# Relative scores of two chunks from one PSUM bank in an attention and expert kernel

## The chip, the cores and the metric

The kernel runs on one core of a Trainium2 chip. The metric is device time in microseconds, the median of several executions. The core has a matmul engine (PE, with its weight loads shown apart as PEld), a vector engine (DVE), an activation engine (ACT), GpSimd (POOL), and a sync engine (SP) which here only issues DMAs. PE writes its results to PSUM, which has eight banks of 128 partitions x 512 fp32 values; DVE and ACT read them out ("drain" them) to SBUF.

## The reference, cut to what matters

The input is x of 2 x 2048 tokens by 256, in fp32. After a layer norm there are two branches, multiplied with each other and added to x. One is attention with relative positions, the other a layer of eight experts, one of which is chosen per token.

```python
q = proj(Wq, bq); k = proj(Wk, bk); v = proj(Wv, bv)     # 16 heads of 16
idx = jnp.clip(r[None, :] - r[:, None], -M, M) + M       # M = 128
content  = einsum('bhqd,bhkd->bhqk', q, k)
relative = einsum('bhqd,qkd->bhqk', q, rel_k[idx])
w = softmax((content + relative) / sqrt(hd))
s = (einsum('bhqk,bhkd->bhqd', w, v)
     + einsum('bhqk,qkd->bhqd', w, rel_v[idx])) @ Wo.T + bo
g = silu(experts(xn))
return x + s * g
```

The relative part depends on key minus query alone, and is constant where the distance is 128 or more.

## The kernel before

**Stages.** The kernel first does the layer norm, the choice of experts and the projections (to about 160 us), storing q, k and v in HBM. Then it runs the experts in blocks of 256 tokens (to about 504 us). The rest is attention. Its order is written out by hand: the pools are under `manual_schedule`, and each engine does its instructions in the order in which the code issues them.

**Chunks and units.** A chunk is 128 queries of a group of four heads; there are 128 chunks (`NCH`). Four chunks in a row are a unit, of which there are 32 (`NU`). The four heads of a group lie on the four 32-row groups of PE's array, so that a matmul with 32 rows for each of the four heads can run side by side.

**Band and far keys.** For a chunk, the keys of the chunk before, its own and the next (three blocks of 128) are the band, in which the distance can be less than 128. All other keys are far: there the relative part is one of two constants, which extra rows of q and k add inside the matmul. Far scores of a unit are cut into tiles of at most 512 query columns (`far_tiles`, 13 or 14 per unit); `far_scores` makes one, ACT takes its exponential (line 824), and `far_values` multiplies it with v into the bank `av`.

**The path of the relative scores.** For each chunk and head `rel_scores` (line 616) multiplies q with `relk_t`, a table of 512 columns whose first and last 128 repeat the end values, less a constant, so that the first 128 products are zero. The matmul takes the other 384 columns. A DVE copy (line 632) drains each bank into `qr`. When the four heads of a chunk are there, one DMA writes `qr` to HBM (`qr_d`, line 637) and a second reads it back with a row stride that is one shorter (`r`, line 641), which turns relative distance into key position. `band_scores` (line 650) multiplies q with the band's keys; DVE adds `r` to it, in place, and takes the row maximum (line 666), and line 678 makes the shift of the exponent of it.

**The path of the band's weights.** One chunk later `band_weights` takes the exponentials in `r` on ACT (line 689). POOL then issues two more DMAs which skew the weights back (`w_d`, line 702, and `wr`, line 704). `turn_band` and `turn_rel` transpose 128 x 128 blocks on PE into a bank `mp`, four to a bank, and copy them to SBUF (`wt`, `wrt`); `band_values` multiplies them with v and with `rel_v`. Of the three banks of `turn_band` ACT copies one (line 733) and DVE the others (line 735); of the two of `turn_rel` one each (lines 759 and 761); the result of `band_values` is copied by ACT (line 789). `put_shifts` puts a unit's shifts into rows of q before its far scores. `finish` divides by the sums, multiplies with Wo, and adds up over the four groups of heads.

**Steps.** The loop at the end of `_attention` writes each chunk as a number of steps. In a step each of the four heads issues one score matmul: a relative one, a band one, or else the next far tile of its queue; then come the drains, then the small work hung on that step (`at(k, ...)`), then far values up to a credit (`give_values`).

```python
even = [len(tiles) * (x + 1) // CB - len(tiles) * x // CB for x in range(CB)]
steps = 2 + (even[i] if U > 0 else 3)
rel_at, band_at = (0, 0, 1, 2), tuple(steps - 3 + x for x in (0, 1, 2, 2))
```

**Buffers.** PSUM: five banks for scores (`sps`), one for `av`, two for transposes and the rest (`mps`). SBUF: one buffer for `qr`, three for `r`, 18 for exponentials. The gate of the experts, silu of their output, is worked out by `gate` in chunks 2 to 11, on POOL and ACT, and stored in HBM; its buffers `yt` and `gt2` share a pool of two each.

Of the kernel before, what the change touches and what calls it, by code (L numbers as in the profile page):

```python
# [8 lines left out]
F32 = mybir.dt.float32  # L9
# [7 lines left out]
P = 128  # L17
# [17 lines left out]
def attn_moe_gate_kernel(  # L35
# [69 lines left out]
    wq_t = load("wq_t", [P, ND, D], wq.rearrange("(k p) m -> p k m", p=P))  # L105
    wk_t = load("wk_t", [P, ND, D], wk.rearrange("(k p) m -> p k m", p=P))
    wv_t = load("wv_t", [P, ND, D], wv.rearrange("(k p) m -> p k m", p=P))
    bq_t = load("bq_t", [P, ND], bq)
    bk_t = load("bk_t", [P, ND], bk)
    bvl = load("bvl", [P, HEADS, HD], bv.partition_broadcast(P))  # L110
    rkc = load("rkc", [P, 2], relk_cols)
    rve = load("rve", [P, 2, HD], relv_ends.partition_broadcast(P))

# [15 lines left out]
    with (  # L129
# [5 lines left out]
        tc.tile_pool(name="pps", bufs=4, space=PSUM) as pps,  # L135
    ):
        xnT = ln1.tile([P, ND, T], F32, name="xnT")
        xn = ln1.tile([P, NT, D], F32, name="xn")
# [367 lines left out]
    def _attention(own, again):  # L506
        accp = own.enter_context(tc.tile_pool(name="sacc", bufs=1))
        gop = own.enter_context(tc.tile_pool(name="gout", bufs=2))
        kvp = own.enter_context(tc.tile_pool(name="kv", bufs=2))
        qrp = own.enter_context(tc.tile_pool(name="qr", bufs=1))  # L510
        rp = own.enter_context(tc.tile_pool(name="r", bufs=3))
# [104 lines left out]
        def rel_scores(n, j):  # L616

            ch = chunk_of(n)
            if "qr" not in ch:
                ch["qr"] = qrp.tile([P, HG, 3 * P], F32, name="qr")  # L620
                ch["qrs"] = 0
            ps = sps.tile([P, TB], F32, name="sp")
            nc.tensor.matmul(  # L623
                ps[:, : 3 * P],
                lhsT=ch["un"]["q"][32 * j : 32 * j + 32, chunk(ch["i"])],
                rhs=relk_t[32 * j : 32 * j + 32, P:],
                start=True,
                stop=True,
            )

            def drain():
                nc.vector.tensor_copy(ch["qr"][:, j, :], ps[:, : 3 * P])  # L632
                ch["qrs"] += 1
                if ch["qrs"] < HG:
                    return
                d = qr_d[n % 3]
                nc.sync.dma_start(
                    out=d.rearrange("p (j r) -> p j r", r=TB)[:, :, P:], in_=ch["qr"]
                )
                ch["r"] = rp.tile([P, HG, 3 * P], F32, name="r")  # L640
                nc.sync.dma_start(
                    out=ch["r"],
                    in_=bass.AP(
                        d.tensor, d.offset + P - 1, [[HG * TB - 1, P], [TB, HG], [1, 3 * P]]
                    ),
                )

            return drain

        def band_scores(n, j):  # L650
# [67 lines left out]
        def turn_band(n, part):  # L718
# [30 lines left out]
        def turn_rel(n, pair):  # L749
# [4 lines left out]
            for jj in range(2):  # L754
                for a in range(2):
                    nc.tensor.transpose(ps[:, jj, a, :], ch["wr"][:, 2 * pair + jj, chunk(a)], ident)  # L756
            dst = ch["wrt"][:, 2 * pair : 2 * pair + 2, :, :]
            if pair == 0:
                nc.scalar.copy(dst, ps)
            else:  # L760
                nc.vector.tensor_copy(dst, ps)

        def band_values(n):
# [23 lines left out]
            for a in range(2):  # L787
                add(lambda j: rvd[:, a, :], lambda j: ch["wrt"][:, j, a, :], stop=(a == 1))
            nc.scalar.copy(un["band"][:, chunk(ch["i"])], ps)
            del chunks[n]  # L790
# [140 lines left out]
        for drain in [rel_scores(0, j) for j in range(HG)]:  # L931
            drain()

        values = []
# [9 lines left out]

        def give_values(share):
# [14 lines left out]
        while n < NCH or values or any(queues) or n <= NCH + 2 * CB + 1:  # L960
# [3 lines left out]
            if i == 0 and 0 < U <= NU:  # L964
                tiles = far_tiles(U - 1)
                for t in tiles:
                    exs = {}
                    for j in range(HG):
                        queues[j].append((U - 1, t, exs, step + 2, t is tiles[-1]))
                even = [len(tiles) * (x + 1) // CB - len(tiles) * x // CB for x in range(CB)]  # L970
# [159 lines left out]
```

## Time and profile before

| | |
|---|---|
| median of 3 runs | 2462.15 us (2458.62 to 2464.61) |
| profiled execution | 2431.08 us |
| its span, first to last instruction | 2429.4 us |
| mean granted PE clock | 0.978 |
| busy: PE, PEld | 2308.6 us, 1446.7 us |
| busy: ACT, DVE, POOL | 1403.8, 993.3, 415.4 us |
| moved by DMA | 498.66 MB, 205 GB/s |

A profile is one execution. Each group of its instructions has a line of the kernel, an engine, an operation and its tiles (out<-in); a number and a mean duration follow. Matmuls are pipelined and their ends are modelled, so "busy" of PE is not work at its peak. An fp32 matmul stands as two instructions. A wait is put down to the instruction that released it. Where the text gives a stretch of time, it is in microseconds from the start of the span.

### The profile page before, as it was taken

The numbers are of one execution on the slowest core, as the hardware profiler recorded it, in microseconds if no ns is written. First come the engines' busy times: TensorE is split into PE (matmuls) and PEld (weight loads), VectorE is DVE, ScalarE is ACT, GpSimd is POOL, SyncE is SP. The second block draws the span as 40 slices with busy tenths as digits, with TensorE's granted clock in tenths as the row PEclk, the third lists the DMA queues.
The fourth block names the chain that finished last, engine by engine and source line by source line (L and its number), as shares of the span: only waits on it lengthen the run. The fifth ranks groups of instructions, "written<-read, shape, count | busy, mean of one in ns | idle before, by whom it ended". The sixth has DMA issues, their size and how long they took to land.

```text
span 2429.4 us, 59289 instructions
## 1 busy us (share of the span) xinstructions
PE 2308.6 (95%) x24522; PEld 1446.7 (60%) x24522; DVE 993.3 (41%) x2533; ACT 1403.8 (58%) x2791; POOL 415.4 (17%) x580
## 2 busy tenths in 40 slices
PE   6989999969999999999999999999999999999996
PEld 5558888844555555556555555555555555655553
DVE  5210000024444554445545544554555445545441
ACT  2211111115666777777667776776777677766774
POOL 3500000005431111111111122211111111111121
PEclk8989999978999999999999999999999999999998
DMA  6765555548765665576656676766666566656652
GB/s 211 224 187 177 185 179 176 167 137 263 248 211 194 218 228 202 195 229 216 203 194 213 241 240 222 244 220 210 207 212 219 196 221 213 219 195 204 215 198 75
DMA packets 272295, 498.66 MB, mean 205 GB/s; under 512 B 33456, under 2 KB 219600, under 8 KB 271504
## 3 DMA queue, kind: packets, MB, share of 16 engines
q1 hardware_dynamic: 218784, 304.67, 38.9%
q0 software_dynamic: 40720, 178.05, 21.2%
q10 hardware_dynamic: 12512, 12.06, 1.4%
q8 instruction: 195, 3.19, 0.6%
q14 instruction: 84, 0.69, 0.1%
HBM read 254.33 MB, written 240.39 MB: 204 GB/s over the span
## 4 chain that ended last, share of the span: by engine, by line
PE 88%; DMA 4%; DVE 3%; issue 2%; ACT 1%; POOL 1%; SPq 0%; DVEq 0%; POOLq 0%; ACTq 0%
PE sp L814 26%; PE av L834 15%; PE mp L775 7%; PE hp L476 7%; PE mp L730 7%; PE yp L487 7%; PE mp L756 5%; PE sp L656 3%; PE mp L899 2%; PE pp L317 2%; PE sp L623 2%; DVE qr L632 1%; PE pp L345 1%; DMA qr_d<-qr 1%; DMA r<-qr_d 1%
## 5 line engine op out<-in xcount | busy, mean ns | idle before, releaser
L824 ACT ACTIVATE ex<-sp 128x512 f32<-128x512 f32 (+1 forms) x1728 | 900.6, 588 | 500.3 <-PE sp L814 461.9
L814 PE MATMUL sp<-q,kT 32*128 32x512 f32 (+7 forms) x4096 | 833.6, 557 | 1.4 <-DVE qr L632 1.4
L666 DVE CUSTOM_DVE_ANT_0 r<-sp,r 128x384 f32<-128x384 f32 (+1 forms) x512 | 266.0, 539 | 538.6 <-PE sp L814 487.4
L814 PEld LDWEIGHTS sp<-q,kT 31*128 31x128 f32 (+1 forms) x4096 | 329.2, 184 | 209.5 <-issue 144.6
L834 PE MATMUL av<-ex,v 128*17 128x256 f32 (+2 forms) x7168 | 421.4, 367 | 0.0
L632 DVE COPY qr<-sp 128x384 f32<-128x384 f32 x512 | 272.6, 554 | 311.0 <-PE sp L814 265.4
L623 PE MATMUL sp<-relk_t,q 32*128 32x384 f32 x1024 | 372.6, 548 | 13.4 <-DVE stat L666 10.5
L656 PE MATMUL sp<-kT,q 31*128 31x384 f32 (+1 forms) x1024 | 356.6, 530 | 3.4 <-DVE qr L632 3.1
L834 PEld LDWEIGHTS av<-ex,v 128*17 128x17 f32 (+1 forms) x7168 | 190.5, 97 | 215.0 <-issue 108.7
L689 ACT ACTIVATE r<-r,shift 128x384 f32<-128x384 f32 (+1 forms) x512 | 294.4, 602 | 19.2 <-DVE shift L678 19.2
L730 PEld LDWEIGHTS mp<-ident,r 128*128 128x128 f32 x1472 | 159.8, 142 | 167.0 <-issue 101.0
L730 PE MATMUL mp<-ident,r 128*128 128x128 f32 x1472 | 218.1, 284 | 16.2 <-ACT r L689 16.1
L704 POOL DMA_DIRECT2D wr<-w_d x128 | 97.5, 762 | 694.6 <-PE sp L814 138.0
L483 ACT ACTIVATE hT<-hp 128x512 f32<-128x512 f32 x92 | 54.9, 597 | 271.8 <-PE hp L476 271.7
L702 POOL DMA_DIRECT2D w_d<-r x128 | 71.1, 555 | 636.9 <-ACT r L689 629.7
L476 PE MATMUL hp<-xsT,w_t 128*128 128x256 f32 x736 | 165.9, 384 | 6.0 <-DVE xsT L470 6.0
L735 DVE COPY wt<-mp 128x512 f32<-128x512 f32 x240 | 164.0, 683 | 10.7 <-PE mp L730 7.4
L487 PE MATMUL yp<-w_t,hT 128*128 128x256 f32 x736 | 162.6, 379 | 0.0
L756 PEld LDWEIGHTS mp<-ident,wr 128*128 128x128 f32 x1024 | 111.4, 142 | 79.9 <-issue 52.3
L476 PEld LDWEIGHTS hp<-xsT,w_t 128*128 128x128 f32 x736 | 140.4, 192 | 27.9 <-DVE xsT L470 8.6
L756 PE MATMUL mp<-ident,wr 128*128 128x128 f32 x1024 | 142.5, 283 | 10.3 <-DMA wr<-w_d 8.9
L487 PEld LDWEIGHTS yp<-w_t,hT 128*128 128x128 f32 x736 | 140.0, 190 | 18.9
(162 smaller groups left out, 2005.4 us busy)
## 6 DMA issues: line engine op xcount, KB each, us to landing
qr_d<-qr SPq DMA_DIRECT2D x128, 768.0 KB
r<-qr_d SPq DMA_DIRECT2D x128, 768.0 KB
w_d<-r POOLq DMA_DIRECT2D x128, 768.0 KB, 5.3
wr<-w_d POOLq DMA_DIRECT2D x128, 512.0 KB, 4.6
w_t<-in_w_dram SPq DMA_DIRECT2D x46, 1024.0 KB
xs_d<-zrow SPq DMA_DIRECT2D x23, 256.0 KB
xs<-xs_d ACTq DMA_DIRECT2D x23, 256.0 KB
ys_d<-ys ACTq DMA_DIRECT2D x23, 256.0 KB
```

Of the source, the lines that this page charges most:

```text
L476: nc.tensor.matmul(ps[:, n, :], lhsT=w1_t[:, k, (h + n) * P : (h + n + 1) * P], rhs=xsT[:, k, :], start=(k == 0), stop=(k == ND - 1),)
L487: nc.tensor.matmul(yp[:, a, :], lhsT=hT[:, h, a * P : (a + 1) * P], rhs=w2_t[:, h, :], start=(h == 0), stop=(h == NH - 1),)
L623: nc.tensor.matmul(ps[:, : 3 * P], lhsT=ch["un"]["q"][32 * j : 32 * j + 32, chunk(ch["i"])], rhs=relk_t[32 * j : 32 * j + 32, P:], start=True,
L632: nc.vector.tensor_copy(ch["qr"][:, j, :], ps[:, : 3 * P])
L656: nc.tensor.matmul(ps[:, :bw], lhsT=ch["un"]["q"][32 * j : 32 * j + RIGHT, chunk(ch["i"])], rhs=ch["gr"]["kT"][32 * j : 32 * j + RIGHT, ch ...
L666: nc.vector.tensor_tensor_reduce(out=r, in0=ps[:, :bw], in1=r, scale=1.0, scalar=LOW, op0=ALU.add, op1=ALU.max, accum_out=stat[:, n, j, 0:1],)
L689: nc.scalar.activation(r[:, j, f0 * P : f1 * P], r[:, j, f0 * P : f1 * P], AF.Exp, bias=shifts[n % (2 * CB)][:, j, ONE : ONE + 1],)
L730: nc.tensor.transpose(ps[:, x, :], ch["r"][:, j, chunk(f0 + f)], ident)
L756: nc.tensor.transpose(ps[:, jj, a, :], ch["wr"][:, 2 * pair + jj, chunk(a)], ident)
L814: nc.tensor.matmul(ps[:, at : at + e - a], lhsT=kT[32 * j : 32 * j + rows, chunk(kc)], rhs=q[32 * j : 32 * j + rows, a:e], start=True, sto ...
L824: nc.scalar.activation(exs[j][:, :n], ps[:, :n], AF.Exp)
L834: nc.tensor.matmul(un["av"][32 * j : 32 * j + cols, a:e], lhsT=v[:, kc, j, :cols], rhs=exs[j][:, at : at + e - a], start=False, stop=False ...
```

## The change

1. `rel_scores` is done for two chunks at a time. It now multiplies each chunk's q with 256 columns of `relk_t`, P to 3P, and puts the products of the two chunks into the two halves of one bank; one DVE copy drains both. It is issued at even chunks for the two chunks after the next, at steps 4, 1, 2, 3 for the four heads.
2. A new function `to_keys` fills the last 128 columns of each head in `qr` with a repeat of the column before them, on DVE, and then issues the two DMAs. It stands at step 0 of the chunk before.
3. `qr` holds two chunks and has two buffers.
4. The number of steps is changed: 2 plus far tiles at even chunks, 1 plus far tiles at odd ones. The band's matmuls stand in the last four steps, one head each. The credits of far values and the place of `load_q` are adapted.
5. DVE does the copies of turned blocks and of `band_values` that ACT did.
6. The weights of the projections, their biases and `rkc` are loaded into the pool `ln1`, which ends with the first stage; only `rve` stays in `const`. The gate's `gt2` gets a pool of one buffer.

```diff
-    def load(name, shape, src):
-        t = const.tile(shape, F32, name=name)
+    def load(name, shape, src, pool=const):
+        t = pool.tile(shape, F32, name=name)
...
-    rve = load("rve", [P, 2, HD], relv_ends.partition_broadcast(P))
+    rve = const.tile([P, 2, HD], F32, name="rve")
...
+        wq_t = load("wq_t", [P, ND, D], wq.rearrange("(k p) m -> p k m", p=P), ln1)
...
+        nc.gpsimd.dma_start(out=rve, in_=relv_ends.partition_broadcast(P))
...
+        gpp = own.enter_context(tc.tile_pool(name="gprod", bufs=1))
-        qrp = own.enter_context(tc.tile_pool(name="qr", bufs=1))
+        qrp = own.enter_context(tc.tile_pool(name="qr", bufs=2))
...
-            gt = gop.tile([P, CB * D], F32, name="gt2")
+            gt = gpp.tile([P, CB * D], F32, name="gt2")
...
             if "qr" not in ch:
-                ch["qr"] = qrp.tile([P, HG, 3 * P], F32, name="qr")
-                ch["qrs"] = 0
+                ch["qr"] = qrp.tile([P, 2, HG, 3 * P], F32, name="qr")
+                chunk_of(n + 1)["qr"] = ch["qr"]
             ps = sps.tile([P, TB], F32, name="sp")
-            nc.tensor.matmul(
-                ps[:, : 3 * P],
-                lhsT=ch["un"]["q"][32 * j : 32 * j + 32, chunk(ch["i"])],
-                rhs=relk_t[32 * j : 32 * j + 32, P:],
...
+            for x in range(2):
+                nc.tensor.matmul(
+                    ps[:, 2 * x * P : 2 * (x + 1) * P],
+                    lhsT=ch["un"]["q"][32 * j : 32 * j + 32, chunk(ch["i"] + x)],
+                    rhs=relk_t[32 * j : 32 * j + 32, P : 3 * P],
...
             def drain():
-                nc.vector.tensor_copy(ch["qr"][:, j, :], ps[:, : 3 * P])
...
+                nc.vector.tensor_copy(
+                    ch["qr"][:, :, j, : 2 * P], ps.rearrange("p (x r) -> p x r", x=2)
                 )
+        def to_keys(n):
+            ch = chunk_of(n)
+            qr = ch["qr"][:, n % 2, :, :]
+            nc.vector.tensor_copy(
+                qr[:, :, 2 * P :], qr[:, :, 2 * P - 1 : 2 * P].to_broadcast([P, HG, P])
+            )
+            d = qr_d[n % 3]
+            nc.sync.dma_start(out=d.rearrange("p (j r) -> p j r", r=TB)[:, :, P:], in_=qr)
+            ch["r"] = rp.tile([P, HG, 3 * P], F32, name="r")
+            nc.sync.dma_start(out=ch["r"], in_=bass.AP(
...
-            if part == 1:
-                nc.scalar.copy(dst, ps)
-            else:
-                nc.vector.tensor_copy(dst, ps)
+            nc.vector.tensor_copy(dst, ps)
...
+            nc.vector.tensor_copy(ch["wrt"][:, 2 * pair : 2 * pair + 2, :, :], ps)
...
-            nc.scalar.copy(un["band"][:, chunk(ch["i"])], ps)
+            nc.vector.tensor_copy(un["band"][:, chunk(ch["i"])], ps)
...
+        to_keys(0)
...
-            credit = min(credit + share, 8 * P)
+            credit = min(credit + columns, 10 * P)
...
+                share = (3, 4, 3, len(tiles) - 10)
...
-                steps = 2 + (even[i] if U > 0 else 3)
-            rel_at, band_at = (0, 0, 1, 2), tuple(steps - 3 + x for x in (0, 1, 2, 2))
+                steps = (2 - i % 2) + (share[i] if U > 0 else 3 + i % 2)
+            rel_at = (4, 1, 2, 3) if n % 2 == 0 and n + 2 < NCH else [None] * HG
+            band_at = range(steps - HG, steps)
...
-                at(2, load_q, U + 1)
+                at(0, load_q, U + 1)
...
-                at(4, turn_rel, n - 2, 0)
-                at(4, turn_rel, n - 2, 1)
+                at(min(4, steps - 1), turn_rel, n - 2, 0)
+                at(min(4, steps - 1), turn_rel, n - 2, 1)
+            if n + 1 < NCH:
+                at(0, to_keys, n + 1)
...
-                    if n + 1 < NCH and k == rel_at[j]:
-                        filled.append((1, j, rel_scores, (n + 1, j), None))
+                    if k == rel_at[j]:
+                        filled.append((1, j, rel_scores, (n + 2, j), None))
...
-                    give_values((5 if k == 1 else 7) * P)
+                    give_values((6 if k == 1 else 8) * P)
```

More of the change, by code (lines that the diff above doesn't have):

```diff
@@ L98, in attn_moe_gate_kernel @@
         nc.vector.memset(rank[:, e : e + 1], float(E - e))
-    def load(name, shape, src):
-        t = const.tile(shape, F32, name=name)
+    def load(name, shape, src, pool=const):
+        t = pool.tile(shape, F32, name=name)
         nc.gpsimd.dma_start(out=t, in_=src)
         return t
[L105 to L111, printed above, removed]
-    rve = load("rve", [P, 2, HD], relv_ends.partition_broadcast(P))
+    rve = const.tile([P, 2, HD], F32, name="rve")
     NE = T // TE + E - 1
@@ L136, in attn_moe_gate_kernel @@
     ):
+        wq_t = load("wq_t", [P, ND, D], wq.rearrange("(k p) m -> p k m", p=P), ln1)
+        wk_t = load("wk_t", [P, ND, D], wk.rearrange("(k p) m -> p k m", p=P), ln1)
+        wv_t = load("wv_t", [P, ND, D], wv.rearrange("(k p) m -> p k m", p=P), ln1)
+        bq_t = load("bq_t", [P, ND], bq, ln1)
+        bk_t = load("bk_t", [P, ND], bk, ln1)
+        bvl = load("bvl", [P, HEADS, HD], bv.partition_broadcast(P), ln1)
+        rkc = load("rkc", [P, 2], relk_cols, ln1)
+        nc.gpsimd.dma_start(out=rve, in_=relv_ends.partition_broadcast(P))
         xnT = ln1.tile([P, ND, T], F32, name="xnT")
@@ L619, in rel_scores @@
             if "qr" not in ch:
-                ch["qr"] = qrp.tile([P, HG, 3 * P], F32, name="qr")
-                ch["qrs"] = 0
+                ch["qr"] = qrp.tile([P, 2, HG, 3 * P], F32, name="qr")
+                chunk_of(n + 1)["qr"] = ch["qr"]
             ps = sps.tile([P, TB], F32, name="sp")
-            nc.tensor.matmul(
-                ps[:, : 3 * P],
-                lhsT=ch["un"]["q"][32 * j : 32 * j + 32, chunk(ch["i"])],
-                rhs=relk_t[32 * j : 32 * j + 32, P:],
-                start=True,
-                stop=True,
-            )
@@ L631, in drain @@
-            def drain():
[L632 to L645, printed above, removed]
-                )
@@ L648, in rel_scores @@
-            return drain
+            for x in range(2):
[3 more added lines that the diff above has]
+                    rhs=relk_t[32 * j : 32 * j + 32, P : 3 * P],
+                    start=True,
+                    stop=True,
+                )
+            def drain():
+                nc.vector.tensor_copy(
+                    ch["qr"][:, :, j, : 2 * P], ps.rearrange("p (x r) -> p x r", x=2)
+                )
@@ new lines, in rel_scores @@
+            return drain
+        def to_keys(n):
[3 more added lines that the diff above has]
+                qr[:, :, 2 * P :], qr[:, :, 2 * P - 1 : 2 * P].to_broadcast([P, HG, P])
+            )
+            d = qr_d[n % 3]
+            nc.sync.dma_start(out=d.rearrange("p (j r) -> p j r", r=TB)[:, :, P:], in_=qr)
+            ch["r"] = rp.tile([P, HG, 3 * P], F32, name="r")
+            nc.sync.dma_start(
+                out=ch["r"],
+                in_=bass.AP(
+                    d.tensor, d.offset + P - 1, [[HG * TB - 1, P], [TB, HG], [1, 3 * P]]
+                ),
+            )
@@ L756, in turn_rel @@
                     nc.tensor.transpose(ps[:, jj, a, :], ch["wr"][:, 2 * pair + jj, chunk(a)], ident)
[L757 to L761, printed above, removed]
+            nc.vector.tensor_copy(ch["wrt"][:, 2 * pair : 2 * pair + 2, :, :], ps)
         def band_values(n):
@@ L943, in halves, with give_values @@
                     yield kc, a + x, min(a + x + w, e), rows, at + x
-        def give_values(share):
+        def give_values(columns):
             nonlocal credit
-            credit = min(credit + share, 8 * P)
+            credit = min(credit + columns, 10 * P)
             while values and values[0][3] <= step and 2 * credit >= values[0][1][2] - values[0][1][1]:
@@ L969, in _attention @@
                         queues[j].append((U - 1, t, exs, step + 2, t is tiles[-1]))
-                even = [len(tiles) * (x + 1) // CB - len(tiles) * x // CB for x in range(CB)]
+                share = (3, 4, 3, len(tiles) - 10)
             if not live:
```

## The prediction

> **What bounds the kernel now.** I read the page first, then windows over units (four chunks each, cut where `put_shifts` runs, line 714), then PE's timeline inside a unit, then the rows of the operations that the change touches.
>
> ```profile
> PE 2308.6 (95%) x24522; PEld 1446.7 (60%) x24522; DVE 993.3 (41%) x2533; ACT 1403.8 (58%) x2791; POOL 415.4 (17%) x580
> PE 88%; DMA 4%; DVE 3%; issue 2%; ACT 1%; POOL 1%; SPq 0%; DVEq 0%; POOLq 0%; ACTq 0%
> ```
>
> PE is the busiest engine and 88% of the chain that ended last. Attention runs from 504 to 2418 us. Two neighbouring units:
>
> ```profile
> 810.99:867.95 56.96, 56.50 (x687) 32.07 (x686) 28.89 (x72) 40.00 (x83) 8.34 (x13) 1.00 0.72 229
> 867.95:924.18 56.23, 55.52 (x711) 33.39 (x709) 28.69 (x72) 40.34 (x80) 8.35 (x13) 1.00 0.61 209
> ```
>
> Columns: length of the stretch, then busy us of PE, weight load, DVE, ACT, POOL, then the granted clock. PE is busy 55.5 of 56.2 us at full clock; ACT has 40 us of work and DVE 29. So PE's own queue is the limit, and another engine matters only where it holds a PSUM bank that PE wants. From the third on, units take 56.2 to 57.0 us, every fourth 59.9.
>
> Inside a unit the PE timeline shows "steps": four heads' score matmuls side by side, then other work:
>
> ```profile
> 901.46 1.09 PE L730 MATMUL mp<-ident,r 128*128 128x128 f32 x8
> 902.48 0.69 PE L814 MATMUL sp<-q,kT 32*128 32x512 f32 x1
> 902.49 0.59 PE L656 MATMUL sp<-kT,q 31*128 31x384 f32 x1
> 902.49 0.89 PE L814 MATMUL sp<-q,kT 32*128 32x512 f32 x2
> 903.74 1.06 PE L834 MATMUL av<-ex,v 128*18 128x256 f32 x16
> 904.73 0.69 PE L814 MATMUL sp<-q,kT 32*128 32x512 f32 x1
> 905.79 0.44 PE L756 MATMUL mp<-ident,wr 128*128 128x128 f32 x2
> ```
>
> A step that waits for nothing runs from 904.73 to 905.79: 1.06 us, whatever its narrower members are (median over the 456 steps of eight score instructions, cut from the timeline: 1.07). Steps whose four members are all 384 wide take 0.84, so 128 columns are worth 0.23 us only if all four heads lose them. The step from 902.48 to 903.74 took 1.26: its fourth tile waited for a bank. ACT drains a step's banks only after the step:
>
> ```profile
> 901.55 1.08 ACT L824 ACTIVATE ex<-sp 128x512 f32<-128x512 f32 x2 [1.47 <-PE sp L814]
> ```
>
> The step before had ended at 901.46; its second exponential ended at 902.63, and with five banks in rotation the new step's fourth tile needs the third bank of the old one: 0.15 us late. So the first drain begins 0.1 us after a step and each takes 0.54. In the tail all four tiles of a step go to ACT, and the wait is larger:
>
> ```profile
> 2367.63 1.06 PE L834 MATMUL av<-ex,v 128*17 128x256 f32 x16
> 2368.62 1.85 PE L814 MATMUL sp<-q,kT 31*128 31x512 f32 x8
> 2370.40 1.09 PE L756 MATMUL mp<-ident,wr 128*128 128x128 f32 x8
> 2371.42 1.06 PE L834 MATMUL av<-ex,v 128*17 128x256 f32 x16
> 2372.41 1.14 PE L814 MATMUL sp<-q,kT 31*128 31x512 f32 x8
> ```
>
> With 0.99 us of other work after a four-tile step the next step takes 1.78 (2368.62 to 2370.40); with 2.01 us it takes 1.07.
>
> **The change part by part.** The sum is made against the profiled execution, 2431.08 us (span 2429.4), which is 1.3% under the median of the three runs, 2462.15. What I get is scaled by 1.0128 at the end.
>
> *Fewer steps.* Each head's row group has one slot per step. Before, a unit needs 4 slots for `rel_scores`, 4 for `band_scores` and 13 or 14 for far tiles (14 where the four chunks lie at an end of the sequence): 21 or 22 steps, as the code's `steps` gives. After, one `rel_scores` serves two chunks: 2 slots, so 19 or 20. The first unit has no far tiles and 20 steps in both. 31 units x 2 = 62 steps x 1.07 us = 66 us off PE's queue. Far tiles, far values and turns keep their number.
>
> *Split relative matmul.* 512 matmuls of 384 columns become 512 of 256, two to a bank. Row first: steps of 12 score instructions in place of 8 (a tile of two pieces) have a median of 1.08 against 1.07, so 0.01 to 0.02 us each; 4 such steps x 62 pairs x 0.015 = 4 us. The Trainium skill, TensorEngine Tiling (Array Packing), section Instruction Overhead, speaks against splitting: about 60 cycles for every matmul, 25 ns at 2.4 GHz. By it, an estimate, two more instructions per head (a matmul is two) put 0.05 us on the step, 12 us in all. I take the row's 4.
>
> *Copies on DVE.* Durations:
>
> ```profile
> L632 DVE COPY qr<-sp 128x384 f32<-128x384 f32 x512 | 272.6, 554 | 311.0 <-PE sp L814 265.4 <-PE sp L623 22.5 <-DMA qr_d<-qr 15.4
> L761 DVE COPY wrt<-mp 128x512 f32<-128x512 f32 x128 | 88.5, 692 | 71.9 <-ACT ex L824 39.5 <-PE mp L756 28.6 <-ACT wrt L759 3.8
> L759 ACT COPY wrt<-mp 128x512 f32<-128x512 f32 x128 | 76.3, 596 | 13.8 <-PE mp L756 7.2 <-issue 5.3 <-ACT ex L824 1.0
> L789 ACT COPY band<-mp 128x128 f32<-128x128 f32 x128 | 34.6, 270 | 27.4 <-PE mp L775 24.1
> L409 DVE COPY kT<-ones_r 128x2048 f32<-128x2048 f32 x2 | 2.5, 1225 | 0.0
> L867 DVE COPY recw<-rec 128x512 f32<-128x512 f32 x1 | 0.6, 570 | 0.0
> ```
>
> Per unit DVE loses 16 x 0.554 = 8.9 us and gains 8 drains of 512 elements at 0.69 (5.5), four copies of the clamped columns in `to_keys` at 0.57 (2.3), and the three kinds of turned copies: 4 x 0.69 + 4 x 0.69 + 4 x 0.28 (6.6). It goes from 28.7 to 34.2 us of about 54.5; ACT from 40.3 to 34.5 (less 4 x 0.59, 4 x 0.60, 4 x 0.27). Neither fills the unit; the cover is PE's 54. Were it gone, DVE's 5.5 us per unit would cost 170.
>
> The `to_keys` copy is SBUF to SBUF with a repeated column, which no row shows in this shape. Nearest: L867, a repeated operand of 512 elements, 570 ns; L409 ran at half that per element. Bounds 0.33 and 0.57; I take 0.57. A rule weighs against it: the Trainium skill, SBUF — State Buffer, section Who interferes with whom, says that a single-source fp32 copy within SBUF may take both of DVE's ports and then locks GpSimd out, with the descriptors of DMAs issued from it. L409's rate fits that, L867's doesn't. By the rule `w_d` or `wr` could be held 0.57 us per chunk, 73 us if all of it reached the end; by the trace POOL is busy 8.4 of 56 us per unit, and PE waited 8.9 us for `wr` in the whole run, in the units with gates. I take 0; ends 0 and +10.
>
> *Which banks wait.* I follow PE with the drain times above. The first step of a chunk now holds four far tiles (except in the four-step chunks), all drained by ACT: the banks come free 0.64, 1.18, 1.72 us after it ends, and the next step needs the third. The small work between is 1.0 us in chunks 2 and 3 of a unit (turn 0.5, `finish` 0.5), 1.5 in chunk 1, over 2 in chunk 0. In chunk 2 this is 0.7 late. In chunk 1 and 3 the transposes before it wait 0.2 for their own two buffers, because both `turn_rel` copies now stand behind two drains on DVE (step end + 0.1 + 0.69 + 0.64 + 0.16 + 0.69 = 2.28 against PE's 2.25, then 2.97 against 2.75); that makes chunk 1 free of a bank wait and leaves 0.47 in chunk 3, 0 where it has four steps. The steps after `turn_band` and after `turn_rel` are 0.16 late each, as in the trace of before: 8 x 0.16 = 1.3. Sum per unit 0.7 + 0.24 + 0.44 + 1.3 = 2.7. Before: 24.04 us in 21 steps, less 21 x 1.07, is 1.6; and in chunk 0 the turn at 868.45 took 1.31 instead of 0.5, waiting for a transpose buffer, 0.8, which the new order does not have. 2.7 - 2.4 = 0.3 x 31 = +8 us, uncertain by 1 us per unit either way (-25 to +40).
>
> *The round trip through HBM.* `to_keys(n+1)` now stands at step 0 of chunk n, where the last drain stood at step 2. On SP the order within a step changes: q loads (eight DMAs, 2.7 us of issue) and k and v loads of the same step now stand ahead of the write, `finish`'s loads and the output store behind it.
>
> ```profile
> 988.79 0.52 SPq L637 DMA_DIRECT2D qr_d<-qr  x1
> 992.76 0.36 SPq L641 DMA_DIRECT2D r<-qr_d  x1
> ```
>
> 4.0 us from write to read, then some 5.3 to landing. After: the copy ends 3.0 us into the chunk, r lands at 12.6. The add to the band scores wants it at 17.2 (chunk 13.7 + step 0 + step 1), in a four-step chunk at 15. Margin 4.6 and 2.4 us; cost 0. Before there was no such wait either after the first unit. The loads of q and k may run ahead, for their buffers are free by then.
>
> *The first three units.* In unit 0 (503.8 to 557.9, 20 steps, DMA waits, clock 0.63) DVE waited 18.1 us for r and 10.6 of its 15.4 us for the single qr buffer. Two buffers, and two chunks' values from the start, take one of its three serial round trips of 9 us away: -10 (0 to -20). The gate's `gt2` has one buffer now: its tanh on ACT, in front of exponentials, waits for the store of the chunk before. Tanh at 648.9, store issued 661.2, next tanh 662.9: with some 4 us to land this is 2 us late, others just in time: +5 (0 to +20) over seven chunks.
>
> *Weights out of the long-lived pool, `rve` kept.* The same DMAs in the same order on POOL, and the same order on every engine up to the attention: 0.
>
> Sum: -66 + 4 + 8 - 10 + 5 = -59. Profiled 2431 - 59 = 2372; by the median 2462 - 60 = 2402.
>
> **The rivals.**
>
> *Only the columns count.* If row groups ran on across step ends, a removed slot would be worth its columns: 512 fewer per head and unit x 0.23/128 us x 31 = 29 us: 2433. Against it: other work stands between almost all steps (687 groups of score work for 686 steps and a tail). For it: the same number comes out if the four-tile steps cost 0.25 us more each than I say (4 x 31 x 0.25). Chance 0.22.
>
> *More than the sum.* If the bank waits shrink with ACT's lighter load and the first units gain 20: -95, so 2366. Chance 0.12.
>
> *The skewed read comes late, and it is slower.* The place: DVE's add of r (line 666 before) heads its queue; behind it are the relative drains and all turned copies, which now are DVE's alone, so PE loses score banks and transpose buffers together. It decides from 0.5 us past the margin per chunk (59/124), so when the round trip takes 5 us over my 9.6. For it: in the gate units one write took 11.4 us, landings reach 9.5, and an output store on SP waited up to 26.8 us for POOL. Against it: steady round trips are even, and the new order puts the write ahead of that store. At 1 us per chunk: -59 + 124 = +65, 2528. Chance 0.10.
>
> **How the numbers follow.** My forecast has 0.53, around 2402 (2370 to 2430). With the rivals at 0.22, 0.12 and 0.10 and 0.03 for no change, faster by over 0.2% is 0.87, slower 0.10. About 0.2%, 5 us, is what a measurement of this kernel can tell from no change. The range reaches from the larger gain to the smaller with stalls: 2362 to 2448.
>
> **What would show it.** 624 steps instead of 686 and unit lengths near 54.5 us; a median step of 1.07 still; a long step (1.7) after the first of chunk 2; DVE near 34 us per unit and ACT near 34.5; the first unit shorter than 54 us; no wait of the DVE add for r after it. I am wrong if steps lengthen to 1.2 in the median, if PE waits for transposes' copies by DVE for more than 1 us per unit, or if the add waits for the DMA.

## The result, and the profile after

The changed kernel takes 2416.99 us (median of 6 runs, 2413.55 to 2422.72) against 2460.39 for the kernel before (6 runs, 2456.37 to 2465.67): a ratio of 0.9825, 95% interval 0.9805 to 0.9844. The gain is 43 us; 60 were predicted.

First the page of the changed kernel, its busy times and its chain of waits:

```profile
PE 2275.4 (94%) x24522; PEld 1507.2 (63%) x24522; DVE 1131.8 (47%) x2789; ACT 1237.9 (51%) x2407; POOL 419.4 (17%) x580
PE 37%; issue 2%; DVE 2%; DMA 2%; ACT 1%; POOL 0%; SPq 0%; POOLq 0%; DVEq 0%
```

PE's instructions keep their number: one of 384 columns has become one of 256, two to a bank. ACT loses 166 us of work and DVE gains 138.5. The chain adds up to 44% here (88% of PE alone before): it could be followed back through less than half of the span, so its shares can't be set beside those of before. The windows can. These are the two units that answer to the two shown of before (length, busy PE, weight load, DVE, ACT, POOL, clock, DMA share, GB/s):

```profile
824.04:880.64 56.60, 56.12 (x706) 35.06 (x705) 32.95 (x80) 34.52 (x71) 8.40 (x13) 1.00 0.71 228
880.64:934.48 53.84, 53.49 (x694) 34.45 (x693) 32.89 (x80) 35.20 (x68) 8.64 (x13) 1.00 0.60 201
```

They were 56.96 and 56.23. PE is still busy nearly all of a unit at full clock. Two steps have gone from each, 20 for 22 and 19 for 21, at a gain of only 0.36 us in the first and of 2.39 in the second. Over four units in a row, 229.28 us became 223.50 (the lines are under `steps_back` below): 1.45 per unit. One place where the new order gives time back shows on PE's timeline in the second unit:

```profile
907.81 1.38 PE L816 MATMUL sp<-q,kT 32*128 32x512 f32 x8
909.12 0.66 PE L739 MATMUL mp<-ident,r 128*128 128x128 f32 x4
909.62 0.60 PE L862 MATMUL mp<-ident,o 128*128 128x128 f32 x4
910.15 0.69 PE L816 MATMUL sp<-q,kT 32*128 32x512 f32 x1
...
911.65 0.43 PE L777 MATMUL mp<-wm,mass 128*32 128x128 f32 x8
```

The step at 907.81 has four far tiles, all drained by ACT. After 1.03 us of turns the next step runs from 910.15 to 911.65: 1.50 in place of 1.07. The work moved to DVE has these rows (a bank of two chunks, the turned blocks of `turn_rel`, those of `turn_band`):

```profile
L741 DVE COPY wt<-mp 128x512 f32<-128x512 f32 x368 | 243.0, 685 | 55.7 <-PE mp L739 51.7
...
L636 DVE COPY qr<-sp 128x512 f32<-128x512 f32 x256 | 175.0, 686 | 37.9 <-PE sp L816 29.7
...
L763 DVE COPY wrt<-mp 128x512 f32<-128x512 f32 x256 | 164.0, 681 | 19.2 <-PE mp L762 18.9
```

**Two profiles that must not be subtracted.** The profiled execution after took 2413.55 us, only 17.5 less than the 2431.08 of before, while the medians differ by 43. The difference lies before attention, which began at 503.79 us in the profile of before and at 529.07 after. The window from 90 to 100 us, in the profile of before and then after:

```profile
90.00:100.00 10.00, 10.00 (x28) 4.32 (x27) 0.38 (x1) 3.32 (x5) 7.55 (x9) 1.00 0.73 230
```

```profile
90.00:100.00 10.00, 2.12 (x5) 0.68 (x4) 0.00 (x0) 0.69 (x1) 7.56 (x9) 0.92 0.32 126
```

POOL scatters tokens for the experts in both. In the first PE goes on with the projections; in the second it is busy for 2.12 of the 10 us, DMA moves little more than half, and SP's queue of stores stands, as its timeline of the kernel after shows:

```profile
93.29 9.47 SPq L328 DMA_DIRECT2D k_d<-k  x2
117.04 2.09 SPq L363 DMA_DIRECT2D v_d<-vt  x4
```

Nothing is issued for some 14 us after the first of these lines ends, and DVE waits once 37.5 us meanwhile. Counted from the first relative matmul, attention took 1914.6 us before and 1871.8 after, so 42.9 less. That is the whole gain, as far as one profile of each can tell: a second profile of the kernel before has an attention 5 us longer (next section).

### The profile page after: what moved, and what is told of

It reads as the page before. It is cut to its first block, busy times and chain, and to the rows that moved or that the text cites. A ratio compares the mean times of both kernels' runs of the same rounds, so it can differ in the third digit from the quotient of the medians.

```text
span 2411.5 us, 58932 instructions
## 1 busy us (share of the span) xinstructions
PE 2275.4 (94%) x24522; PEld 1507.2 (63%) x24522; DVE 1131.8 (47%) x2789; ACT 1237.9 (51%) x2407; POOL 419.4 (17%) x580
## 5 line engine op out<-in xcount | busy, mean ns | idle before, releaser
L816 PE MATMUL sp<-q,kT 32*128 32x512 f32 (+7 forms) x4096 | 763.3, 558 | 2.9 <-DVE stat L675 1.9
L675 DVE CUSTOM_DVE_ANT_0 r<-sp,r 128x384 f32<-128x384 f32 (+1 forms) x512 | 275.1, 538 | 506.6 <-PE sp L816 306.7
L665 PE MATMUL sp<-kT,q 31*128 31x384 f32 (+1 forms) x1024 | 454.2, 530 | 0.0
L816 PEld LDWEIGHTS sp<-q,kT 32*128 32x128 f32 (+1 forms) x4096 | 301.9, 184 | 193.3 <-issue 138.5
L627 PE MATMUL sp<-relk_t,q 32*128 32x256 f32 x1024 | 287.0, 407 | 19.1 <-DVE stat L675 16.0
L741 DVE COPY wt<-mp 128x512 f32<-128x512 f32 x368 | 243.0, 685 | 55.7 <-PE mp L739 51.7
L627 PEld LDWEIGHTS sp<-relk_t,q 32*128 32x128 f32 x1024 | 169.4, 187 | 41.1 <-DVE stat L675 18.9
L636 DVE COPY qr<-sp 128x512 f32<-128x512 f32 x256 | 175.0, 686 | 37.9 <-PE sp L816 29.7
L763 DVE COPY wrt<-mp 128x512 f32<-128x512 f32 x256 | 164.0, 681 | 19.2 <-PE mp L762 18.9
L497 DVE COPY ys<-yp 128x512 f32<-128x512 f32 x23 | 15.9, 691 | 308.6 <-PE yp L489 308.6
```

The lines of the kernel that those rows point to most:

```text
L627: nc.tensor.matmul(ps[:, 2 * x * P : 2 * (x + 1) * P], lhsT=ch["un"]["q"][32 * j : 32 * j + 32, chunk(ch["i"] + x)], rhs=relk_t[32 * j : 3 ...
L636: nc.vector.tensor_copy(ch["qr"][:, :, j, : 2 * P], ps.rearrange("p (x r) -> p x r", x=2))
L665: nc.tensor.matmul(ps[:, :bw], lhsT=ch["un"]["q"][32 * j : 32 * j + RIGHT, chunk(ch["i"])], rhs=ch["gr"]["kT"][32 * j : 32 * j + RIGHT, ch ...
L675: nc.vector.tensor_tensor_reduce(out=r, in0=ps[:, :bw], in1=r, scale=1.0, scalar=LOW, op0=ALU.add, op1=ALU.max, accum_out=stat[:, n, j, 0:1],)
L763: nc.vector.tensor_copy(ch["wrt"][:, 2 * pair : 2 * pair + 2, :, :], ps)
L816: nc.tensor.matmul(ps[:, at : at + e - a], lhsT=kT[32 * j : 32 * j + rows, chunk(kc)], rhs=q[32 * j : 32 * j + rows, a:e], start=True, sto ...
```

## The experiments

Ratios are to the kernel before, run on the same chip. Parts of attention are cut from PE's timeline, each from the first matmul of a kind to the first of the next; where nothing else is said they are sums over units 3 to 30.

**Is the 29 us at the start a matter of the change?** The kernel before, profiled a second time.

> The kernel before, profiled once more. The changed kernel's attention part took 43 us less than that of the profile before (529.1 to 2400.8 against 503.8 to 2418.4), but its first stages took 25 us more: between 83 and 117 us the stores on SP landed only when the scatter on POOL was through. Theory: this delay is not of the change, and the usual executions of the kernel before (median 2460, against 2431 profiled) have it too; then this profile shows attention starting near 530 and a time near 2460. Rival: moving the weights into the pool ln1 made it; then attention starts near 504 here and the time stays near 2431, and where the runs at 2460 lose 29 us is open.

It took 2465.16 us. Attention began at 532.95 and lasted 1919.5. Its window:

```profile
90.00:100.00 10.00, 5.49 (x21) 3.42 (x19) 0.00 (x0) 0.69 (x1) 7.56 (x9) 0.95 0.35 139
```

So the kernel before has the same delay; the profile that the prediction was made on was an execution without it. The weights' move is not the cause. In all the profiles that follow attention begins late too, between 528.7 and 536.2. Why that one execution escaped stays open.

**Do the steps pay?** The changed kernel with the steps of before.

```diff
-                steps = (2 - i % 2) + (share[i] if U > 0 else 3 + i % 2)
+                steps = 2 + (share[i] if U > 0 else 3)
```

> The changed kernel, but with two slots per chunk besides far tiles in odd chunks too (steps = 2 + share), so 686 steps as before and everything else of the change in place. Theory (a step costs PE its 1.07 us whatever it holds, less what a looser order saves in bank waits): 62 steps x 1.07 = 66 us more, less bank waits of about 0.5 us per unit (16 us) and late reads (8 us), so +42 us, about 2459, near the kernel before. Rival (only the columns count): the columns are those of the changed kernel, so within 5 us of 2417.

2474.66 us, 1.0035 (1.002 to 1.0049). Attention took 1922.4, 50.6 more than the changed kernel. Four regular units in a row, in which no r comes late, in the kernel before, in this one and in the changed one:

```profile
924.18:1153.46 229.28, 224.70 (x2811) 131.52 (x2809) 113.19 (x286) 162.69 (x328) 33.81 (x53) 1.00 0.64 210
```

```profile
948.58:1180.61 232.03, 228.05 (x2809) 142.73 (x2809) 131.59 (x319) 142.06 (x281) 34.52 (x53) 1.00 0.62 208
```

```profile
934.48:1157.98 223.50, 219.89 (x2813) 139.34 (x2809) 130.17 (x318) 141.87 (x280) 34.51 (x53) 1.00 0.66 218
```

Between the last two, eight steps are worth 8.53 us: 1.07 each, net of the waits that change with them, which is what an unhindered step takes. By the columns alone they would be worth nothing here, since the columns did not change. Between the first two, at the same number of steps, the rest of the change costs 2.75 us, 0.69 per unit. So it is not the removal of steps that is paid back in a regular unit, but the new order around it. Over all of attention the 62 steps are worth less, 50.6 / 62 = 0.82 us each. Most of the difference lies in two places: units 1 and 2 are no shorter for four steps fewer (125.3 us against 124.3 here), and the reads of r that come late in the changed kernel after unit 0 (8 us, see below) do not come late here. With the steps back, the kernel is 8 us slower than before.

**Are DVE's copies the reason?** The changed kernel with the copies of `part == 1`, `pair == 0` and `band_values` on ACT again (`copies_back`), and the kernel before with all of them on DVE (`copies_alone`).

```diff
-            nc.vector.tensor_copy(dst, ps)
+            if part == 1:
+                nc.scalar.copy(dst, ps)
+            else:
+                nc.vector.tensor_copy(dst, ps)
...
-            nc.vector.tensor_copy(un["band"][:, chunk(ch["i"])], ps)
+            nc.scalar.copy(un["band"][:, chunk(ch["i"])], ps)
```

> The changed kernel with the copies of the second turned block, the first of turn_rel and the band's result back on ACT. Theory (PE bounds, and ACT holds the score banks): ACT goes from 34.5 to 40 us per unit, but its copies run while PE does other work, except in the chunks whose first step is drained by ACT alone; bank waits grow by about 0.2 us per chunk, so +10 to +25 us. Rival (the copies queued on DVE hold up transposes and drains): it gets faster, by up to 0.25 us per unit = 8 us and the small waits of line 739 for a DVE copy (62 us of PEld's waits, most hidden).

> The kernel before, with the change's copies alone: DVE copies the second turned block, the first of turn_rel and the band's result. DVE goes from 28.7 to about 35.3 us per unit, ACT from 40.3 to 34.5, PE's work is the same. Theory: within 5 us of the kernel before (bank waits of 1.6 us per unit shrink by a third at most, -15 us, and transposes wait 0.2 us more in two chunks of four, +12 us). Rival (ACT's relief is a good part of what the change gained): 15 to 30 us faster than before.

`copies_back`: 2416.71 us, 0.9803 (0.9758 to 0.9847): no different from the changed kernel, and the expected loss did not come. Two things cancel: units 3 to 30 are 10 us shorter with the copies on ACT (1563.5 against 1573.0), units 1 and 2, in which the gates are made, 10 us longer (135.4 against 125.3). In four regular units the copies on ACT take 222.49 in place of 223.50, so 0.25 of the 0.69 us per unit that the rest of the change costs comes with the copies on DVE. `copies_alone`: 2458.51, 0.9982 (0.9967 to 0.9998), 5 us under its own before. Relieving ACT is not what the change gains by.

**Can the bank waits be spread?** The band's matmuls were placed over other steps, so that no step holds four far tiles with little behind it.

```diff
-            rel_at = (4, 1, 2, 3) if n % 2 == 0 and n + 2 < NCH else [None] * HG
-            band_at = range(steps - HG, steps)
+            rel_at = (0, 0, 1, 2) if n % 2 == 0 and n + 2 < NCH else [None] * HG
+            band_at = (0, 2, 3, steps - 1) if i % 2 else (2, 3, 4, 4)
```

> The changed kernel with its slots placed otherwise: at even chunks the relative matmuls at steps 0, 0, 1, 2 and the band's at 2, 3, 4, 4; at odd chunks the band's at 0, 2, 3 and the last. The step of four far tiles then is followed by 2.6 us of other work and not by 1.0. Theory (bank waits behind a step that only ACT drains): the 0.43 and 0.45 us at the second step of chunks 2 and 3 and part of the eight 0.24 us per unit go, 0.9 to 1.5 us per unit, 28 to 45 us, unless r comes late for the band at step 0 of odd chunks: about 2385. Rival (the total of columns and copies decides, not their order): no change beyond 5 us.

2433.81 us, 0.9885 (0.9857 to 0.9912), the wrong way against the changed kernel. The list of waits of its profiled execution, which took 2447.80 us (us in total, times, longest), says why:

```profile
DVE r L675 <- DMA r<-qr_d: 71.1, 29, 6.5
```

Of these, 25 waits and 50 us lie after unit 0, all in odd chunks: there the band now begins at step 0, where r has not landed yet. The margin of the round trip is what this placement spends.

**The round trip a chunk earlier.** One `qr` buffer fewer pays for a fourth `r`, and `to_keys` stands a chunk earlier; alone (`r_early`) and with the spread band (`spread_early`, at step 3 there).

```diff
-        qrp = own.enter_context(tc.tile_pool(name="qr", bufs=2))
-        rp = own.enter_context(tc.tile_pool(name="r", bufs=3))
+        qrp = own.enter_context(tc.tile_pool(name="qr", bufs=1))
+        rp = own.enter_context(tc.tile_pool(name="r", bufs=4))
...
+        to_keys(1)
...
-            if n + 1 < NCH:
-                at(0, to_keys, n + 1)
+            if n + 2 < NCH:
+                at(4 if n % 2 == 0 else 0, to_keys, n + 2)
```

> The changed kernel with the write and read of qr one place earlier: for even chunks at step 4 of the chunk two before (as soon as their last drain is there), for odd chunks a whole chunk earlier than in the change; r has four buffers, and qr one, for room. In the changed kernel's profile DVE waited for r at 1428, 1994 and 2104 us and those units took up to 5 us more than their like (together 8 us over 29 units). Theory (the margin that I had put at 2.4 us in four-step chunks is eaten up where other transfers stand on SP): those waits go, all units of a kind take the same time, -8 us, and the bank waits stay (0.43 and 0.45 us at the second step of chunks 2 and 3): about 2409. Rival (the irregular units are PE or bank waits that only show as a wait for r): irregular units stay, no change.

> The slots of 'spread' (four far tiles only in a step that 2.6 us of other work follows), with r earlier as in 'r_early' (even chunks at step 3). 'spread' itself gave 2434, not 2385: its profile has 29 waits of DVE for r, 71 us in all, and only the units at a sequence's end, where r was not late, were shorter (56.7 for 58.6 us). Theory (bank waits behind a step that ACT alone drains, and in 'spread' late reads hid the gain): no waits for r after the first unit, all units 1 to 2 us shorter than the changed kernel's, 30 to 50 us with the 8 of the late reads: 2367 to 2390. Rival (the order of slots does not matter, 'spread' lost to bank waits that it shifted): no better than 'r_early'.

`r_early`: 2416.87, 0.9835 (0.9797 to 0.9873), the same within the measurement. The late r of the later units is gone, and with it 6.2 us over units 3 to 30 (1566.8 against 1573.0), but units 1 and 2 took 3.6 us more. `spread_early`: 2415.73, 0.9838 (0.9791 to 0.9885), where 30 to 50 us of gain were expected. The score part fell from 666.5 to 639.0, as the theory said; the part of `turn_band` rose from 195.8 to 209.8. Units 3 to 30 came out 15 us shorter than in the changed kernel, but units 0 to 2 took 5.7 more, and in this profile attention began 7 us later. On PE's timeline at the start of a unit:

```profile
1058.96 0.66 PE L723 MATMUL mp<-ident,shift 128*128 128x128 f32 x4
1059.45 0.60 PE L739 MATMUL mp<-ident,r 128*128 128x128 f32 x4
1060.83 1.13 PE L901 MATMUL mp<-wo_t,o 128*128 128x256 f32 x4 [0.78 <-DVE q L725]
```

and on DVE's in the same place:

```profile
1058.88 1.29 DVE L636 COPY qr<-sp 128x512 f32<-128x512 f32 x2
1060.09 0.68 DVE L725 TENSOR_TENSOR q<-mp,q 128x512 f32<-128x512 f32 x1
```

`put_shifts`, `turn_band` and `finish` want a transpose bank one after the other, and there are two. The third must wait until DVE's add (line 725) has read the first, and two relative drains of step 0 stand ahead of that add: from 1059.45 to 1060.83 is 1.38 us for 0.5 of transposes.

**The same with the copies on ACT**, to see whether DVE's load is what keeps the gain away.

> The same as 'spread_early' with the turned copies shared with ACT as before. 'copies_back' was the changed kernel's equal within its interval; in its profile the even units were 0.1 to 0.4 us shorter and the two gate units 10 us longer. Theory (PE bounds; which engine copies the turned blocks matters by tenths of a us per unit): within 10 us of 'spread_early', either way. Rival (ACT's load sets the bank waits): 20 us or more slower than 'spread_early', since 5.8 us per unit go back to ACT.

2415.32, 0.9826 (0.979 to 0.9863). It is not: the part of `turn_band` stays at 209.3, and units 3 to 30 take 6.7 us more.

**No relative drain at step 0.** From `spread_early`:

```diff
-            rel_at = (0, 0, 1, 2) if n % 2 == 0 and n + 2 < NCH else [None] * HG
+            rel_at = (1, 1, 2, 3) if n % 2 == 0 and n + 2 < NCH else [None] * HG
...
-                at(3 if n % 2 == 0 else 0, to_keys, n + 2)
+                at(4 if n % 2 == 0 else 0, to_keys, n + 2)
```

> The kernel with the spread band and the early round trip, but with the relative matmuls at steps 1, 1, 2, 3 in place of 0, 0, 1, 2, and the copy for the chunk after the next at step 4 of even chunks in place of 3. Theory: in the spread kernel two relative drains of 0.69 us stand on DVE in front of the add of put_shifts at step 0 of each unit, and that add holds a transpose buffer which finish wants: PE waits 0.78 us there. With no relative drain at step 0 the transposes (turn_band's part) lose 0.4 to 0.5 us per chunk 0 and some in chunk 2, 14 us over units 3 to 30, while the score part stays within 5 us of 639: about 2402 (ratio 0.976 to 0.980). Rival: the waits only move, since two drains now meet at later steps: the score part grows by 10 or more, and the time stays within 5 us of the spread kernel's 2416.

2403.24 us, 0.975 (0.9723 to 0.9776): faster than before by more than the changed kernel, and the intervals of the two ratios don't touch. PE's timeline at the start of the same unit:

```profile
1050.58 0.60 PE L739 MATMUL mp<-ident,r 128*128 128x128 f32 x4
1051.53 1.13 PE L901 MATMUL mp<-wo_t,o 128*128 128x256 f32 x4 [0.35 <-DVE q L725]
```

0.95 us in place of 1.38. The part of `turn_band` fell to 193.0, somewhat more than expected; but the score part rose to 650.2, which is the rival's "10 or more". So 11.2 of the 16.8 us that the turns gave went back into bank waits: units 3 to 30 took 6.8 us less than in `spread_early`, all of attention 11.7. The time is the theory's, the account between the two parts is shared.

**Early round trip and ACT copies.**

> The kernel with the early round trip (four r buffers, one qr buffer, the copies a chunk earlier), and the turned copies on ACT as before. Theory: what the two edits did by themselves adds up, since they act on different waits: units 3 to 30 took 6 us less with the early round trip and 10 us less with the copies on ACT, and the first unit and the gates' units 4 and 8 us more: about 2413 (ratio 0.979 to 0.983), which is within the measurement of both. Rival: the units with gates carry the loss of the ACT copies for another reason than a late r, and then they stay at 135 us and the time is 2420 or more.

2411.82, 0.9797 (0.9773 to 0.982). The time is the theory's, and units 3 to 30 (1558.6) gain from both edits. But units 1 and 2 are the rival's: 139.4 us, with r in time there. The list of waits for 585 to 722 us, of PE and of ACT, has the reason:

```profile
PE sp L627 <- ACT ex L833: 10.2, 2, 8.7
...
ACT gt L575 <- DMA gate_d<-gt: 11.5, 2, 9.4
```

ACT came to a gate's tanh before the store of the gate before it had landed, and stood 9.4 us; the exponentials behind the tanh then kept PE from its score banks for 8.7. This is the wait that the prediction put on the single `gt2`. In the changed kernel ACT never waits for it.

## Why the prediction was right, and where its steps failed

The direction and the mechanism held: 623 groups of score work in place of 687, a step of 1.07 us, ACT at 34.5 to 35.2 us per unit (34.5 predicted), and the steps put back take all of the gain away. The amount was 17 us too large, and two of the prediction's own signs came out against it: the first unit is not shorter than 54 us (56.6), and the add waits for the DMA after it. By the steps of the prediction, on profiled attention:

| | predicted | measured |
|---|---|---|
| unit 0 | -10 | +2.5 |
| units 1 and 2 | 2 x -1.75 + 5 = +1.5 | -11.7 |
| units 3 to 31, regular | 29 x -1.75 = -51 | 29 x -1.45 = -42 |
| units 3 to 31, late r | 0 | +8 |
| tail | 0 | +0.4 |
| sum | -59 | -42.9 |

Against the second profile of the kernel before, units 1 and 2 would stand at -17.5 and the sum at -47.7. That the total still lies well inside the forecast is in part luck: units 1 and 2 gave 13 us more than was predicted for them, for a reason that the prediction did not have, and without these the gain would be 30 us and the time about 2430, at the edge of the forecast.

**Steps, bank waits and turns (-1.75 per unit).** Two steps less, 2.14 us, were right. In the four regular units (78 steps for 86) the score work over 1.07 per step went from 6.91 to 10.77 us, +0.96 per unit; by the prediction's terms it was 2.26 less 1.6, +0.66. Its place was right: after a step of four far tiles, in chunks 2 and 3 (1.50 us each, where 1.77 and 1.54 were worked out). Two terms were put too low. The small waits that it put at 0.16 were 0.24. It also read eight of them into a unit of before, where only the four steps after `turn_band` were late (1.26 us); those after `turn_rel` took 1.06 to 1.11 and mostly take 1.31 now. The other term is chunk 0. The prediction took out 0.8 us there, "which the new order does not have". It has 0.44 of it:

```profile
1048.03 0.60 PE L739 MATMUL mp<-ident,r 128*128 128x128 f32 x4
1048.97 1.13 PE L901 MATMUL mp<-wo_t,o 128*128 128x256 f32 x4 [0.35 <-DVE q L725]
```

(PE in the changed kernel at the start of a unit: 0.94 where an unhindered turn takes 0.5.) The transpose buffer that PE waits for is held by `put_shifts`' own add, which needs its 0.69 us on DVE in either order. In part these misses were made up: the turns of the other chunks cost about 0.2 us per unit where 0.44 was put, and the far values took 0.18 less.

**Split relative matmul (+4).** Nothing: steps with a split pair take 1.07 to 1.08. The row's estimate was near; the 12 us that the Trainium skill's TensorEngine Tiling (Array Packing), section Instruction Overhead, would give did not appear.

**The clamped copy.** In 118 of 128 cases its 512 elements took 0.41 to 0.43 us where I took 0.57, nearer to the row at half price. The rule of the Trainium skill, SBUF — State Buffer, section Who interferes with whom, would then have DVE and GpSimd lock each other out, and the trace agrees. The other ten copies took 0.48 to 0.93 us. In each of them POOL had begun an instruction before, nine times its issue of `wr`, and the copy ended 0.2 to 0.3 us after that:

```profile
1228.07 0.76 POOL L713 DMA_DIRECT2D wr<-w_d  x1 [4.76 <-PE sp L816]
```

```profile
1228.13 0.93 DVE L646 COPY qr<-qr 128x512 f32<-128x512 f32 x1
```

The other way round, four issues of `wr` that a copy followed after 0.18 to 0.19 us took 0.90 to 0.91 us, where the median is 0.76. In all this is 2.5 us of DVE's time and about 1 us of POOL's in the whole run, and the means of POOL's issues hardly moved (`w_d` 556 ns against 555, `wr` 767 against 762). So the lock is real and far from the 73 us that every chunk's would have made; no cost of it shows in the time, and 0 was right.

**The round trip (0).** This was wrong, and it is the same wrong assumption as in unit 0: that a write and its read take what they took alone. SP's timeline in the changed kernel, for one round trip in unit 0 and one much later:

```profile
558.48 0.52 SPq L650 DMA_DIRECT2D qr_d<-qr  x1
569.25 0.38 SPq L652 DMA_DIRECT2D r<-qr_d  x1
...
1412.57 0.52 SPq L650 DMA_DIRECT2D qr_d<-qr  x1
1420.32 0.36 SPq L652 DMA_DIRECT2D r<-qr_d  x1
```

Write to read is 10.8 and 7.75 us, where the prediction's one pair had 4.0. The one pair was typical of the kernel before, whose 128 pairs have a median of 4.0; in the changed kernel the median is 5.4, and 11 pairs take 7.5 or more. With a margin of 2.4 to 4.6 us that makes r late. DVE's timeline in unit 0, and its line in the list of waits of the whole run:

```profile
555.20 0.42 DVE L646 COPY qr<-qr 128x512 f32<-128x512 f32 x1
567.30 0.56 DVE L675 CUSTOM_DVE_ANT_0 r<-sp,r 128x384 f32<-128x384 f32 x1 [11.69 <-DMA r<-qr_d]
```

```profile
DVE r L675 <- DMA r<-qr_d: 27.2, 6, 11.7
```

Three of the six waits (22.1 us, where before had 18.1) lie in unit 0. Two buffers did end the waits for `qr` there, but two of the first four writes now begin within 1 us of the read of another pair. These two pairs took 6.8 and 10.8 us from write to read, the other two 3.8 and 4.4. That the transfers slow each other is read from this timing, and no run here separates it. `r_early`, which has a single `qr` buffer again, waited 12.6 us for r and 7.2 for `qr` in unit 0, and the unit took 57.2. What makes up the 2.5 us stays open. The other three waits (5.1 us) lengthen units late in the run, one of them from 54.48 to 59.48. `r_early` removes those three, and no unit from 3 to 30 is then more than 0.6 us longer than its like, which shows the cause; it is the rival with the late read, at 8 us of the 124 that it put on it.

**The gates (+5).** The wait is real, as `r_early_act` shows, but not in this kernel, where ACT with less work in a different order reaches each tanh after the store. That units 1 and 2 are shorter by 12 us is a gain that I had not seen. With the band in the last steps they take 124 to 129 us where DVE has the copies (changed kernel, `steps_back`, `r_early`) and 135 to 139 where ACT has them (`copies_back`, `r_early_act`); in the kernel before it was 137 and 143, and 134 with the copies on DVE. So the copies' engine makes some 10 us in the changed kernel's order. It is no rule: with the spread band and the early round trip ACT's copies cost nothing there (127.9 and 126.8). What makes the rest stays open.

**Base and scale.** Multiplying by 1.0128 assumed that the profiled execution was faster all through. It was faster in one place, before attention; this put 1 us on the gain.

The rival with only the columns falls by `steps_back`. The larger gain fell with unit 0 and the bank waits. ACT's lighter load alone does shrink these (in `copies_alone` the score work of four regular units is 97.46 us for 98.93), but the new order of the drains adds more than that.

## What to carry to other kernels

Removing slots from a full engine's queue paid what the slots took, 1.07 us each. What was lost was lost in the order around them: 0.69 us per unit, in waits for banks that one engine drains alone and for transpose buffers. Running the new order with the old number of slots is what told the two apart. When a round trip through HBM is moved, size its margin by the slowest pair in the trace, with another transfer beside it, rather than by one quiet pair. And when the time of a profile is far from the median, find the place where it differs before subtracting two profiles.

## What the runs showed of the hardware

- While POOL scattered tokens (about 83 to 117 us), SP's stores nearly stood still in the profiles of the changed kernel and of the kernel before taken again: DMA share 0.32 and 0.35 in the window shown, and attention 25 to 29 us later. The first execution of the kernel before kept 0.73 and 230 GB/s under the same load of POOL. From 100 to 110 us the share is 0.67 in that execution and 0.25 to 0.33 in the eleven other profiles. What decides between them was not tried.
- A copy within SBUF with a repeated column took 0.42 us for 512 elements, against 0.69 for the same count out of PSUM. Where it began during an issue of `wr` by POOL, it ended some 0.2 us after the issue and took up to 0.93 us.
- After PE had stood 8.7 us for ACT in `r_early_act`, the granted clock was 0.51 from 636 to 640 us and 1.00 from 640 to 644, and score matmuls of 512 columns took 1.05 to 1.21 us in place of 0.69: the stall cost more than its own length.
